# Regrouping the hidden columns of a quantized feed-forward kernel: seven waves of three pairs, the half chunk first in the last one

## The chip, the cores and the metric

The kernel runs on one core of one Trainium2 chip. The metric is the device time of one execution in microseconds (us), as the median of several runs. The core's engines appear under the profile's names: PE (matrix multiplication, with its weight loads as PEld), DVE (VectorE), ACT (ScalarE), POOL (GpSimd) and SP, whose queue issues most of the DMA transfers. PSUM, where matrix products land, has eight banks here, each of 128 partitions by 512 numbers in 32 bits.

## What is computed

The input is 2048 rows of 1024 numbers. Three layers run over it, each with a residual: a feed-forward layer, a state-space layer (a causal convolution along the 1024 numbers of each row), and the same feed-forward layer again. Each normalizes its input first.

```
x = x + 0.5 * ffn(layernorm(x))
x = x + s4(layernorm(x))             # long convolution with a computed response, plus D * u
x = x + 0.5 * ffn(layernorm(x))

ffn(x):  Wg, Wu: 1024 x 2752, Wd: 2752 x 1024, all from 4-bit words:
         W[k, n] = scale[k // 128, n] * (w4[k, n] - (zero[k // 128, n] + 1))
         h = silu(x @ Wg) * (x @ Wu);   out = h @ Wd
```

## The kernel before

**Jobs.** The rows are handled in four blocks of 512, and each block passes the feed-forward layer twice, which makes eight jobs (line 1232). A job runs an up stage, `gate_up` (line 602), then a down stage, `down` (line 678). Job 0 also turns the 4-bit words into bytes in DRAM, which all later jobs load. Job 1 also computes the tables of the convolution.

**Units and waves.** The 2752 hidden columns are 21 chunks of 128 and one half chunk of 64. A chunk has a gate column and an up column, together a pair of units; the half chunk's gate and up columns lie side by side in one unit. That is 43 units, each with a PSUM bank of its own while it is in work. A wave is a set of units that are in work together (`WAVES`, line 37): five waves of three pairs (six banks), two of two pairs (four banks), and one of two pairs and the half unit (five banks).

**Steps.** Each wave goes through the eight groups of 128 input numbers, one step for each, 64 steps in all. In a step every unit gets two products of 128x128 by 128x512 (line 628): one with the high part of the normalized input (32 bits, `xTh`) and one with the low part (16 bits, `xTl`). For the first half of the units the high product comes last, for the others the low one. After a unit's second product its bank is multiplied by the ratio of two groups' scales, in place, by ACT (line 598) for even unit numbers and by DVE (line 600) for odd ones; the half unit alternates between the two by step. The next step's product into that bank waits for this.

**End of a wave.** After a unit pair's last step `gated` (line 651) applies the sigmoid product on ACT (`g`, line 653), multiplies on DVE (`hf`, line 656) and gives both banks back. POOL then splits `hf` into a high part `hh` (line 658) and the rest `hl` (line 660). The pool of `hf` has two tiles (line 101), so a third `hf` waits for the `hl` of the first. `gated_half` (line 663) does the same for the half unit, with two more DVE operations (lines 672 and 673) in place of POOL's.

**Weights.** A step's bytes are loaded by SP (line 558) and turned into 32-bit numbers by POOL (line 576; in job 0 partly by ACT, line 574), some steps ahead: six tiles of bytes, five of weights. In job 0 `dequantize` (line 474) makes the bytes: DVE splits the words of a wave (lines 450 to 463), POOL casts eight tiles `q` from a pool of four (line 99, cast in line 478), and SP stores each of them (line 482). `dequantize_down` (line 506) does so for the down weights with the same pool.

**Down stage.** Four banks `po`, 21 chunks and the half chunk for each half of the outputs: per chunk eight products (line 689), with the banks rescaled in between as above. It takes four banks at its start.

**Hooks.** Other work is tied to step numbers (lines 1234 to 1326): moments and deviations of a normalization (lines 175 and 196, on DVE), transposes (line 219), convolutions (line 961), loads and stores of rows. For a job after a first feed-forward job the convolution of the previous block starts at step 8, in job 1 at step 38. In job 0 the words of wave w are handled from step 8w - 12 (line 520), and those of the down weights from step 52 (line 532).

**Order.** Each engine works through its own fixed order of instructions. The code sets the dependences; a scheduler puts the instructions of each engine in order when the program is built, and assigns tiles and banks. `in_order_of_writing` (line 140) fixes the order of a few pieces.

Of the kernel before, what the change touches and what calls it, by code (L numbers as in the profile page):

```python
# [12 lines left out]
I32 = mybir.dt.int32  # L13
I8 = mybir.dt.int8
U16 = mybir.dt.uint16
F32R = mybir.dt.float32r
# [7 lines left out]
P = 128  # L24
# [7 lines left out]
GK = 8  # L32
GD = 21
TW = 6
WIDE = INTER // P
HALF = INTER - WIDE * P
WAVES = [list(range(3 * w, 3 * w + 3)) for w in range(5)] + [[15, 16], [17, 18], [19, 20]]
STEPS = [(w, g) for w in range(len(WAVES)) for g in range(GK)]
NH = HID // 512
EIGHT = 8.0  # L40
LIFT = 2.0**20
# [13 lines left out]
def macaron_s4_kernel(  # L55
# [31 lines left out]
    nc = tc.nc  # L87
# [5 lines left out]
    small = ctx.enter_context(tc.tile_pool(name="small", bufs=2))  # L93
# [2 lines left out]
    hpool = ctx.enter_context(tc.tile_pool(name="h", bufs=2 * NF))  # L96
    wpool = ctx.enter_context(tc.tile_pool(name="w", bufs=5))
    bpool = ctx.enter_context(tc.tile_pool(name="bytes", bufs=6))
    qpool = ctx.enter_context(tc.tile_pool(name="q", bufs=4))
    gpool = ctx.enter_context(tc.tile_pool(name="g", bufs=3))  # L100
    hfpool = ctx.enter_context(tc.tile_pool(name="hf", bufs=2))
    ypool = ctx.enter_context(tc.tile_pool(name="y", bufs=4))
    ppool = ctx.enter_context(tc.tile_pool(name="ps", bufs=1, space=PSUM))
    dpool = ctx.enter_context(tc.tile_pool(name="dram", bufs=1, space=DRAM))
# [27 lines left out]
    def t2(name, dt=F32):  # L132
        return hpool.tile([P, 512], dt, tag="h", name=name)
# [275 lines left out]
    def units(w):  # L409
# [4 lines left out]
    width_of = lambda w: len(units(w)) * P  # L414
    w_q = [
        dpool.tile([HID, width_of(w)], I8, tag=f"wq{w}", name=f"wq{w}") for w in range(len(WAVES))
    ]
# [130 lines left out]
    loaded, made = {}, {}  # L548

    def load_bytes(i):  # L550
        j, stage, s = queue[i]
        if i == 0:
            loaded[i] = first_tile
            return
        if stage == "up":
            w, g = STEPS[s]
            loaded[i] = t = bpool.tile([P, width_of(w)], I8, tag="b", name=f"b_{j}_{s}")
            nc.sync.dma_start(t, w_q[w][bass.ts(g, P), :])
            return

        a, f = divmod(s, NF)
        loaded[i] = t = bpool.tile([P, 512], I8, tag="b", name=f"bd_{j}_{s}")
        m = width(f)
        for o in range(0, P, m):
            nc.sync.dma_start(t[o : o + m], wd_q[a][f * P : f * P + m, :])

    def make_weights(i):
        j, stage, s = queue[i]
        b = loaded.pop(i)
        made[i] = t = wpool.tile(list(b.shape), F32R, tag="w", name=f"w_{stage}_{j}_{s}")  # L570
        if i == 0:
            nc.vector.tensor_copy(t, b)  # L572
        elif j == 0 and stage == "up" and s % GK in (1, 2, 5):
            nc.scalar.copy(t, b)
        else:
            nc.gpsimd.tensor_copy(t, b)  # L576

    at_use = [0]

    def next_weights():  # L580
        i = at_use[0]
        at_use[0] += 1
        for k in range(LOAD) if i == 0 else ():
            load_bytes(k)
        for k in range(MAKE) if i == 0 else ():
            make_weights(k)
        if i + LOAD < len(queue):
            load_bytes(i + LOAD)
        if i + MAKE < len(queue):
            make_weights(i + MAKE)  # L590
        return made.pop(i)
# [10 lines left out]
    def gate_up(j, b, hooks):  # L602
        hi, lo = pieces[b]
        ps = {}
        for s, (wi, g) in enumerate(STEPS):
            w = next_weights()
            for hook in hooks.get(s, ()):
                hook()
            fs = WAVES[wi]
            n = len(fs)  # L610
            order = [(2 * f + i, i * n + u) for u, f in enumerate(fs) for i in range(2)]
            if wi == len(WAVES) - 1:
                order.append((2 * WIDE, 2 * n))


            early = len(order) // 2
            turns = [(k, pos, k == 1) for k in range(2) for pos in range(early)]
            turns += [(k, pos, k == 0) for k in (1, 0) for pos in range(early, len(order))]
            for k, pos, done in turns:
                unit, col = order[pos]  # L620
                if g == 0 and unit not in ps:
                    ps[unit] = acc(f"pg_{j}_{unit}")
                p = ps[unit]
                weights = w[:, bass.ts(col, P)]
                if k == 0:

                    weights = weights.bitcast(BF16).rearrange("p (n k) -> p k n", k=2)[:, 1, :]
                nc.tensor.matmul(  # L628
                    p,
                    weights,  # L630
                    (lo, hi)[k][:, g, :],
                    start=(g == 0 and not done),
                    stop=(g == GK - 1 and done),
                    skip_group_check=True,
                )
                if not done:
                    continue
                if g < GK - 1:
                    on_act = unit % 2 == 0 or (j == 0 and pos == 1 and g % 4 == 0)
                    if unit == 2 * WIDE:  # L640
                        on_act = g % 2 == 0
                    scaled(on_act, p, p, rat[:, unit, g : g + 1])
                elif unit == 2 * WIDE:
                    gated_half(j, ps[unit])
                    give_back(ps.pop(unit))
                elif unit % 2:
                    gated(j, unit // 2, ps[unit - 1], ps[unit])
                    give_back(ps.pop(unit - 1), ps.pop(unit))
        pieces.pop(b)
# [372 lines left out]
    def general():  # L1022
# [22 lines left out]
        def gather_table(dst, s_dram, z_dram, groups, n, name):  # L1045


            s = t4(f"s_{name}")[:, :n]
            nc.gpsimd.memset(s, 0.0)
            for k in range(3):  # L1050
                nc.sync.dma_start(s[32 * k : 32 * k + groups, :], s_dram)
            z = small.tile([P, P], I32, tag="z", name=f"z_{name}")[96:P, : n // 8]
            nc.gpsimd.memset(z, 0)
            nc.sync.dma_start(z[:groups, :], z_dram)
            zi = s[96:P, :].bitcast(I32).rearrange("p (a k) -> p k a", k=8)
            for k in range(8):
                nc.vector.tensor_scalar(
                    zi[:, k, :], z, 4 * k, 15, ALU.logical_shift_right, ALU.bitwise_and
                )
            nc.vector.tensor_scalar(dst[96:P, :], s[96:P, :].bitcast(I32), 1.0, None, ALU.add)  # L1060
            nc.vector.tensor_copy(dst[0:96, :], s[0:96, :])
            for k in range(1, 3):
                for lo in range(k, 3):
                    rows = slice(32 * lo, 32 * lo + 32)
                    nc.vector.tensor_tensor(s[rows, :], s[rows, :], dst[rows, :], ALU.subtract)
                    nc.vector.tensor_copy(dst[rows, :], s[rows, :])
# [167 lines left out]
    def fast():  # L1234
        for j, (b, k) in enumerate(JOBS):
            prev = JOBS[j - 1] if j else None
            after = JOBS[j + 1] if j + 1 < len(JOBS) else None
            up, dn = {}, {}

            def at(hooks, s, f):  # L1240
                hooks.setdefault(s, []).append(f)

            if prev:
                pb, pk = prev
                for t in range(NT):
                    at(up, t, lambda t=t: back(pb, 1, t))
                if pk == 1:
                    late = 30 if j == 1 else 0
                    at(up, 4, lambda: moments(pb, 2))
                    at(up, 5, lambda: deviations(pb, 2))  # L1250
                    s4x, s4n = {}, {}

                    def norm(t):
                        s4n[t] = normalized(pb, t)

                    def swap(t):
                        s4x[t] = turn_whole(s4n.pop(t), f"st_{pb}_{t}")

                    def conv(t):
                        convolve(pb, t, s4x.pop(t), f"{pb}_{t}")  # L1260

                    for t in range(NT):
                        at(up, late + 8 + 4 * t, lambda t=t: norm(t))
                        at(up, late + 10 + 4 * t, lambda t=t: swap(t))
                        at(up, late + 12 + 4 * t, lambda t=t: conv(t))
                    at(up, late + 27, lambda: moments(pb, 3))
                    at(up, late + 28, lambda: deviations(pb, 3, LIFT))

                    def save():
                        for t, dst in enumerate(saved(pb)):  # L1270
                            nc.sync.dma_start(dst, x[pb][t])

                    at(up, late + 28, save)
                else:

                    def store():
                        for t, dst in enumerate(rows_of(out, pb)):
                            nc.sync.dma_start(dst, x[pb][t])
                        x.pop(pb)

                    at(up, 4, store)
# [190 lines left out]
```

## Time and profile before

| what | value |
|---|---|
| median of 3 runs | 2197.08 us (2196.97 to 2197.81) |
| the profiled execution | 2195.57 us |
| its span, first to last instruction | 2193.7 us |
| mean granted PE clock | 0.993 |
| PE busy | 2119.6 us, 97% |
| DVE, ACT, POOL busy | 78%, 64%, 46% |
| DMA queue q1, share of 16 engines | 19.4% |
| one product in the up stage (line 628): 5504 of them | mean 444 and 384 ns from start to end, high and low part |
| POOL cast of a step's weights, 768 / 640 / 512 columns | 841 / 750 / 618 ns |

The profile is one execution, so its own time of 2195.57 us is what sums made from it are compared with; it lies 1.5 us under the median. A product's duration runs from its start to the end of its result and overlaps its neighbours: on a PE without waits the next product starts about 0.22 to 0.23 us later, and a PE that looks busy can still lose time. Where a stage's pace matters, starts are compared, not durations. "Idle before" in a list of groups names what ended an engine's idle time; on an engine that isn't the bottleneck such idle time costs nothing.

### The profile page before, as it was taken

Reading aid. Unit: us, or ns where it says so; the run is one execution under the profiler, and the core shown is the slowest. Engines: PE = TensorE matmul, PEld = TensorE weight load, DVE = VectorE, ACT = ScalarE, POOL = GpSimd, SP = SyncE. Lnnn points to the kernel's source line nnn. Section 1 sums busy time; section 2 is a strip of 40 time slices with the busy share of each in tenths; the row PEclk is TensorE's granted clock in tenths of the full one; section 3 lists DMA queues with packets and bytes.
Section 4 is the critical chain, followed back from the end, with each engine's and each line's share of the span. In section 5 each row is a group of like instructions: output and inputs, shape, how many; then the busy total and the mean of one; then the engine's idle time right before and its main releaser. Section 6 shows DMA issues by size and latency. Waiting matters only on the chain.

```text
span 2193.7 us, 29717 instructions
## 1 busy us (share of the span) xinstructions
PE 2119.6 (97%) x9524; PEld 1421.1 (65%) x9524; DVE 1720.4 (78%) x2826; ACT 1404.9 (64%) x2197; POOL 1015.0 (46%) x1334
## 2 busy tenths in 40 slices
PE   5999899999999999999999999999999999999998
PEld 3555665566867568655775558676686766865576
DVE  7889889778887877778777787867778677777776
ACT  5877466446754677666767667646776466767765
POOL 3868734444334453455334553435534345345642
PEclk9999999999999999999999999999999999999999
DMA  4433321112111211211321121112111121121111
GB/s 139 120 96 111 105 69 32 54 49 74 38 40 46 93 45 46 79 34 33 107 71 46 31 71 35 41 51 72 37 34 42 49 93 36 54 81 36 33 33 57
DMA packets 163681, 132.43 MB, mean 60 GB/s; under 512 B 22395, under 2 KB 151172, under 8 KB 163518
## 3 DMA queue, kind: packets, MB, share of 16 engines
q1 hardware_dynamic: 162670, 129.12, 19.4%
q8 instruction: 77, 1.26, 0.2%
q10 hardware_dynamic: 592, 1.25, 0.1%
q14 instruction: 86, 0.70, 0.1%
q0 software_dynamic: 256, 0.10, 0.0%
HBM read 104.79 MB, written 25.50 MB: 59 GB/s over the span
## 4 chain that ended last, share of the span: by engine, by line
PE 84%; DVE 7%; POOL 4%; issue 2%; DMA 1%; SPq 1%; ACT 0%; POOLq 0%; DVEq 0%; ACTq 0%
PE pg L628 50%; PE po L689 26%; PE pc L987 3%; DVE pg L600 2%; PE pc L968 1%; PE pb L711 1%; POOL hl L660 1%; PE pt L219 1%; DVE po L600 1%; DVE hf L656 1%; POOL w_up L576 1%; PE st L219 1%; POOL w_down L576 1%; POOL hh L658 1%; DVE rawd L461 0%
## 5 line engine op out<-in xcount | busy, mean ns | idle before, releaser
L598 ACT ACTIVATE pg<-pg,rat 128x512 f32<-128x512 f32 x1224 | 778.6, 660 | 472.3 <-PE pg L628 471.3
L600 DVE TENSOR_TENSOR pg<-pg,rat 128x512 f32<-128x512 f32 x1184 | 788.0, 694 | 167.5 <-PE pg L628 163.2
L628 PE MATMUL pg<-xTh,w_up 128*128 128x512 f32 x2752 | 878.5, 444 | 11.9 <-DVE pg L600 9.4
L628 PE MATMUL pg<-xTl,w_up 128*128 128x512 f16 x2752 | 731.1, 384 | 14.7 <-DVE w_up L572 6.6
L576 POOL CAST w_up<-b 128x768 fp32r<-128x768 int8 (+2 forms) x487 | 376.0, 774 | 614.0 <-PE pg L628 470.6
L628 PEld LDWEIGHTS pg<-xTh,w_up 128*128 128x128 f32 x2752 | 519.7, 190 | 203.0 <-DVE pg L600 41.7
L689 PE MATMUL po<-hl,w_down 128*128 128x512 f32 x1344 | 540.6, 405 | 15.4 <-DVE po L600 9.7
L598 ACT ACTIVATE po<-po,ratd 128x512 f32<-128x512 f32 x640 | 421.4, 662 | 175.1 <-PE po L689 175.1
L689 PE MATMUL po<-hh,w_down 128*128 128x512 f32 x1344 | 523.6, 393 | 0.0
L600 DVE TENSOR_TENSOR po<-po,ratd 128x512 f32<-128x512 f32 x640 | 441.6, 698 | 93.6 <-PE po L689 89.1
L628 PEld LDWEIGHTS <-w_up 128*128 128x128 bf16 x2752 | 228.3, 99 | 344.1 <-issue 165.2
L576 POOL CAST w_down<-bd 128x512 fp32r<-128x512 int8 x352 | 220.6, 628 | 422.3 <-PE po L689 366.2
L689 PEld LDWEIGHTS po<-hl,w_down 128*128 128x128 f32 x1344 | 252.9, 189 | 94.1 <-DVE po L600 23.9
L689 PEld LDWEIGHTS po<-hh,w_down 128*128 128x128 f32 x1344 | 254.0, 189 | 46.0
L660 POOL TENSOR_TENSOR hl<-hf,hh 128x512 fp32r<-128x512 f32 x168 | 218.0, 1297 | 7.9
L656 DVE SCALAR_TENSOR_TENSOR hf<-pg,rat,g 128x512 f32<-128x512 f32 x168 | 124.2, 749 | 86.7 <-ACT g L653 44.6
L653 ACT ACTIVATE g<-pg,rat 128x512 f32<-128x512 f32 x168 | 111.0, 687 | 45.9 <-PE pg L628 36.3
L658 POOL CAST hh<-hf 128x512 fp32r<-128x512 f32 x168 | 104.7, 623 | 61.4 <-PE pg L628 41.1
L182 DVE BATCH_NORM_STATS2 stats<-x 128x6 f32<-128x512 f32 x96 | 63.6, 677 | 1.0
L219 PE MATMUL pt<-ident,xn 128*128 128x128 f32 x256 | 44.2, 293 | 10.3 <-ACT xn L1339 7.6
L242 DVE TENSOR_TENSOR xTl<-pt,xTh 128x512 f16<-128x512 f32 x56 | 38.3, 688 | 13.7 <-ACT xTh L241 12.9
L219 PEld LDWEIGHTS pt<-ident,xn 128*128 128x128 f32 x256 | 34.8, 151 | 21.1 <-ACT xn L1339 9.2
(163 smaller groups left out, 957.2 us busy)
## 6 DMA issues: line engine op xcount, KB each, us to landing
b<-wq SPq DMA_DIRECT2D x319, 96.0 KB
bd<-wdq SPq DMA_DIRECT2D x336, 64.0 KB
x<-in_L_attn_u_dram SPq DMA_DIRECT2D x30, 512.0 KB
b<-wq SPq DMA_DIRECT2D x128, 64.0 KB
xs<-x SPq DMA_DIRECT2D x16, 512.0 KB
x<-xs SPq DMA_DIRECT2D x16, 512.0 KB
out_dram<-x SPq DMA_DIRECT2D x16, 512.0 KB
b<-wq SPq DMA_DIRECT2D x64, 80.0 KB
```

The source lines that it names most:

```text
L182: nc.vector.bn_stats(stats[:, t, i, :], x[b][t][:, bass.ts(i, 512)])
L219: nc.tensor.transpose(ps[:, bass.ts(k, P)], n[:, bass.ts(k, P)], ident)
L576: nc.gpsimd.tensor_copy(t, b)
L598: nc.scalar.activation(dst, src, AF.Copy, scale=sc)
L600: nc.vector.tensor_tensor(dst, src, sc.to_broadcast([P, TB]), ALU.mult)
L628: nc.tensor.matmul(p, weights, (lo, hi)[k][:, g, :], start=(g == 0 and not done), stop=(g == GK - 1 and done), skip_group_check=True,)
L653: nc.scalar.activation(g, pg, AF.Silu, scale=rat[:, 2 * f, GK - 1 :])
L656: nc.vector.scalar_tensor_tensor(hf, pu, last, g, ALU.mult, ALU.mult)
L658: nc.gpsimd.tensor_copy(hi, hf)
L660: nc.gpsimd.tensor_tensor(lo, hf, hi.bitcast(F32), ALU.subtract)
L689: nc.tensor.matmul(ps[c], w[:, bass.ts(c, P)], part, start=(f == 0 and k == 0), stop=(f == NF - 1), skip_group_check=True,)
L987: nc.tensor.matmul(dst, lhsT, rhs, start=start, stop=stop, skip_group_check=True)
```

## The change

The 21 pairs are taken as seven waves of three. The last wave also has the half unit, so it holds seven banks, and the half unit is the first in its order instead of the last. A step's weight tile then has at most 768 columns, also in the last wave: the half unit's weights for all eight steps come from one further load and two POOL casts into tiles of their own (`half_weights`), asked for twelve steps before the end of the up stage. There are 56 steps in place of 64.

The pool of `hf` gets a third tile. The pool of `q` loses one of four. The step numbers of the hooks follow: in job 1 the convolution starts at step 33 with a tile every three steps, in the other jobs the moments after it come at step 26 in place of 27. Job 0's words are handled from step 8w - 12 as before, now of seven waves, and those of the down weights from step 44. A small tile of the fallback path, which isn't taken here, moves to another pool.

```diff
-WAVES = [list(range(3 * w, 3 * w + 3)) for w in range(5)] + [[15, 16], [17, 18], [19, 20]]
+WAVES = [list(range(3 * w, 3 * w + 3)) for w in range(7)]
...
-    qpool = ctx.enter_context(tc.tile_pool(name="q", bufs=4))
+    qpool = ctx.enter_context(tc.tile_pool(name="q", bufs=3))
...
-    hfpool = ctx.enter_context(tc.tile_pool(name="hf", bufs=2))
+    hfpool = ctx.enter_context(tc.tile_pool(name="hf", bufs=3))
...
             w, g = STEPS[s]
-            loaded[i] = t = bpool.tile([P, width_of(w)], I8, tag="b", name=f"b_{j}_{s}")
-            nc.sync.dma_start(t, w_q[w][bass.ts(g, P), :])
+            n = 2 * P * len(WAVES[w])
+            loaded[i] = t = bpool.tile([P, n], I8, tag="b", name=f"b_{j}_{s}")
+            nc.sync.dma_start(t, w_q[w][bass.ts(g, P), :n])
...
+    def half_weights(j):
+
+        b = t2(f"b_half_{j}").bitcast(I8)[:, : GK * P].rearrange("p (g n) -> p g n", g=GK)
+        rows = w_q[-1][:, -P:].rearrange("(g k) n -> k g n", k=P)
+        nc.sync.dma_start(b, rows)
+        got = []
+        for i in range(2):
+            t = t2(f"w_half_{j}_{i}", F32R)
+            t = t.rearrange("p (g n) -> p g n", g=4)
+            nc.gpsimd.tensor_copy(t, b[:, 4 * i : 4 * i + 4])
+            got += [t[:, g] for g in range(4)]
+        return got
...
             w = next_weights()
+            if s == len(STEPS) - GK - 4:
+                half = half_weights(j)
...
             if wi == len(WAVES) - 1:
-                order.append((2 * WIDE, 2 * n))
+                order.insert(0, (2 * WIDE, None))
...
-                weights = w[:, bass.ts(col, P)]
+                weights = half[g] if col is None else w[:, bass.ts(col, P)]
...
-            z = small.tile([P, P], I32, tag="z", name=f"z_{name}")[96:P, : n // 8]
+            z = t2(f"z_{name}").bitcast(I32)[96:P, : n // 8]
...
-                    late = 30 if j == 1 else 0
+                    o, gap = (33, 3) if j == 1 else (8, 4)
...
-                        at(up, late + 8 + 4 * t, lambda t=t: norm(t))
-                        at(up, late + 10 + 4 * t, lambda t=t: swap(t))
-                        at(up, late + 12 + 4 * t, lambda t=t: conv(t))
-                    at(up, late + 27, lambda: moments(pb, 3))
-                    at(up, late + 28, lambda: deviations(pb, 3, LIFT))
+                        s = o + gap * t
+                        at(up, s, lambda t=t: norm(t))
+                        at(up, s + 2, lambda t=t: swap(t))
+                        at(up, s + 4, lambda t=t: conv(t))
+                    done = o + 3 * gap + 6
+                    at(up, done, lambda: moments(pb, 3))
+                    at(up, done + 1, lambda: deviations(pb, 3, LIFT))
...
-                    at(up, late + 28, save)
+                    at(up, done + 1, save)
```

## The prediction

> **What bounds the kernel now.** I read the page's first and fourth parts, then the stretches of some stages, then the chain of waits at two wave ends. The page says that PE carries the time:
>
> ```profile
> span 2193.7 us, 29717 instructions
> ...
> PE 2119.6 (97%) x9524; PEld 1421.1 (65%) x9524; DVE 1720.4 (78%) x2826; ACT 1404.9 (64%) x2197; POOL 1015.0 (46%) x1334
> ...
> PE 84%; DVE 7%; POOL 4%; issue 2%; DMA 1%; SPq 1%; ACT 0%; POOLq 0%; DVEq 0%; ACTq 0%
> ```
>
> The change keeps all 5504 up products and 2752 down products. So only PE's stalls can give anything: the 7% of DVE and 4% of POOL in the chain, some 240 us at the very most, much of it in the starting phase and in job 0. The stretches say where. Cut at product starts, they are: job 7's fifth wave; its last three waves; its first 32 down products; then the last three waves of job 4 and of job 0.
>
> ```profile
> core 0: us, PE busy (x) PEld busy (x) DVE busy (x) ACT busy (x) POOL busy (x), PEclk, DMA share, GB/s
> 2028.78:2050.61 21.83, 21.83 (x98) 13.02 (x96) 16.03 (x25) 15.26 (x25) 11.12 (x15) 1.00 0.09 25
> 2050.61:2098.54 47.93, 47.42 (x209) 27.80 (x208) 35.19 (x52) 33.94 (x53) 27.98 (x38) 1.00 0.13 35
> 2098.54:2108.06 9.52, 8.77 (x34) 5.78 (x33) 7.96 (x12) 6.05 (x10) 6.19 (x8) 1.00 0.09 26
> 1251.24:1302.33 51.09, 49.43 (x210) 26.69 (x208) 44.59 (x81) 33.42 (x53) 28.95 (x38) 1.00 0.24 75
> 150.24:204.90 54.66, 51.43 (x218) 27.34 (x216) 48.98 (x76) 40.10 (x66) 46.00 (x63) 1.00 0.47 140
> ```
>
> The same 208 products take 47.93 us in job 7, 51.09 in job 4 and 54.66 in job 0. The chain at job 7's change from the fifth to the sixth wave (start, us, engine, tile) shows the mechanism:
>
> ```profile
> 2050.82 0.38 POOL hh L658
> 2051.20 0.56 POOL w_up L576
> 2051.76 1.25 POOL hl L660
> ...
> 2053.03 0.75 DVE hf L656
> 2053.78 0.62 DVE pg L600
> ```
>
> The third `hf` finds both tiles taken, waits for POOL's `hl` of the first, and holds DVE's queue; the rescaling behind it comes late, and the product after it starts 0.90 us after its predecessor instead of 0.23. The list of waits on `hf` counts 37 waits for POOL's `hl`, 37.5 us. At the down start `hf_half` is caught likewise:
>
> ```profile
> 2101.46 0.76 DVE hf_half L670
> ...
> 2102.25 0.71 DVE po L600
> ...
> 2102.98 0.64 DVE hb L672
> ...
> 2103.65 0.71 DVE po L600
> ```
>
> **What the skill says.** Perfetto Trace Analysis, Optimization Strategy: the same gap repeating on the engine that should be saturated can mean that SBUF or PSUM ran out for the next tile. The trace agrees: the gap of 0.9 us recurs at the same wave change of jobs 2, 3, 4, 5, 6 and 7. TensorE: Matmul & The Clock Gate, its specification table, calls the VectorE and ScalarE queues strict FIFO; the trace agrees, a blocked `hf` delays the `pg` behind it. DMA: Bandwidth & Descriptors, Specifications, asks for 512 B or more per transfer for line rate; the new half load moves runs of 128 B, and no row of before shows such a load.
>
> **Part 1, wave shapes, quiet jobs 2, 5, 6, 7.** In the timeline a six-unit step's 12 products take 2.70 us (first low products at 2041.86, 2044.55, 2047.25), so 0.225 each. Eight steps make 21.58; the fifth wave took 21.83, so a change between three-pair waves costs 0.25. After: one such wave, 21.6, and eight steps of 14 products, 8 x 14 x 0.225 = 25.2, plus 0.25: 47.0 against 47.93. **Gain 0.9 x 4 = 3.6 us** (0 to 4.5). This needs a last wave that isn't starved of banks. Walked through with the durations above: from the start of the sixth wave's last step, `hf` 15, 16, 17 end at 2.76, 3.51, 4.26 us (with three tiles none waits for POOL), and the new wave wants their banks at 3.14 to 4.72 us. The tightest margin is 0.46 us. With two tiles the third would miss it.
>
> **Part 2, jobs 3 and 4.** Here moments and deviations at steps 44 and 45 put about 10 us on DVE (44.59 against 35.19 busy), and the stretches are 50.32 and 51.09. In jobs 5 and 6 the same work lies in a three-pair wave and costs nothing there (21.6 us for either wave): a bank has 8 product slots between its last product and its next, against 5 in a two-pair wave. After, step 44 lies in a three-pair wave, but the tail reaches the tight last wave. I take 47.0 + 1.5 = 48.5 (47.3 to 50): 1.8 + 2.6 = **4.4 us** (1.5 to 6.5).
>
> **Part 3, down starts, jobs 1 to 7.** The first 32 products take 9.52 us in job 7 and 10.13 to 10.21 in jobs 1 to 6, which also hold eight transposes; 32 x 0.228 + 0.2 for the first is 7.5, so 2.1 is stall. In the built program's order after, DVE does `hf_half`, `hf` 18, `hb`, `hf` 19, `hb`, `hf` 20, then `po`: 0.76 + 0.75 + 0.64 + 0.75 + 0.81 + 0.75 = 4.46 us ahead of the first `po`. `hf_half` can start 1.82 us into the last step (its product comes first, and the sigmoid takes 0.69), so that `po` ends at about 7.0; PE, which starts down at 3.15, wants it at 5.9. Stall 1.1 in place of 2.1, 0.7 to 1.0 where transposes fill it. **Gain 1.0 x 7 = 7 us** (2 to 9). POOL's order (three `hh`, `hl` pairs, 5.7 us, between `w_down` casts) serves each cast over 2 us early.
>
> **Part 4, job 1.** Its last three waves take 79.54 us with four convolutions. In job 5 two waves with four take 74.3, 30.7 over two plain ones, so 48.8 are left here: 0.9 over job 7, 1.8 over 47.0. The `hf` wait also sits in its chain at the fourth wave's end (`hl` 1.68 us, then no product until 425.75), some 1.5 us, and I add 1.2 for stalls around the table work, since its whole up stage takes 24.1 us more than job 5's (213.7 against 189.6) and the table products only some 12 of these. Convolutions now come at steps 37 to 46; the table they need was ready at 430.8 us, about step 35, so they don't wait. **Gain 4.5 us** (2 to 8), the down start apart.
>
> **Part 5, job 0.** DVE is 90% and POOL 84% busy in its last stretch. Three `hf` tiles, longer steps and the earlier split of the last words (DVE) help, perhaps 4 us of the 6.7 over job 7. Against it stands the smaller `q` pool: a cast of 0.84, an issue of 0.33 and a landing of 2.0 us (both from the rows of `q`) are 3.2 us; with four tiles that is 0.80 per cast, no slower than the cast, with three 1.06. Over 48 casts on POOL 0.22 x 48 = 10.6 us, which POOL's gaps in the earlier waves cover (busy 14 to 19 of 22 to 24 us per wave); uncovered it costs up to 10. **Gain 2 us** (-6 to +7).
>
> **Moved at no cost.** Half load and casts: per job one load and 2 x 0.62 on POOL; but 16 x 0.84 + 1.24 = 14.7 us replaces 16 x 0.62 + 8 x 0.75 = 15.9, and POOL idles 20 of 47.93 us. In the built order the load stands ahead of that for step 51 and the casts beside those for steps 46 and 47, so even a doubled landing of 4 us holds only casts that are more than two steps early; if not, about 3 us per job. SP issues 17 loads in place of 24. One spare bank in the last wave instead of three: no hook there takes one in the built order. Wider tiles keep each load's runs at 768 B.
>
> **Sum.** 3.6 + 4.4 + 7 + 4.5 + 2 = 21.5. From the profiled 2195.57 (span 2193.7 and 1.9 around it) that gives 2174.1; the median lies 1.5 higher, so 2175.6, and I say **2175**.
>
> **Rivals.** *Half eaten:* the last wave holds seven of eight banks, so any DVE lateness over 0.46 us goes to PE at its start, and in jobs 0, 1, 3, 4 DVE is late. Parts 2, 4, 5 give a third of 10.9, part 3 half: 3.6 + 3.6 + 3.5 = 10.7, so 2186. For it: DVE's 44.59 of 51.09; against: the built order runs ACT's units ahead there. *No change:* a product that PE starts earlier waits at the next rescaling, since DVE at 78% paces it: 2197. Against: the waves without stalls run at 0.225 with the same DVE share. *Slower:* the `q` ring of three in job 0. If every cast of `q` and of the down words (0.61 + 0.33 + 2.0 over 3 is 0.98 against 0.61, so 0.37 x 48 = 17.8) pays in full, 10.6 + 17.8 = 28.4 eats 23.5 of gains elsewhere with some left: about 2202. It decides once casts come more than three in a row with POOL as the limit, as from 225 to 270 us, where POOL is busy 37.82 of 45. *Larger:* job 0 gains 15 us and job 1 8: 21.5 + 13 + 3.5 = 38, so 2159; for it, DVE's 90% there, against, its work stays.
>
> **Chances.** Forecast 0.60, half eaten 0.20, no change 0.06, slower 0.07, larger 0.07. Range 2160 to 2192: it leaves out the slower and unchanged cases and most of the larger, 0.2. The forecast's own range is 2163 to 2184. A difference under 0.2% (4.4 us) is about what a measurement can't tell from none: faster 0.87, same 0.06, slower 0.07.
>
> **What would show it.** After: `hf` no longer waits for `hl`; the last two waves of job 7 take 47.0 us, of job 4 about 48.5; the first 32 down products 8.6 in job 7 and 9.2 in job 3; POOL's `q` waits for stores without PE waiting for `w_up`. Wrong if products at the last wave's start wait for a bank, or if job 0 grows.

## The result, and the profile after

The changed kernel takes 2183.39 us (median of 4 runs, 2179.01 to 2185.12), the kernel before on the same chip 2197.02: a ratio of 0.9939, 95% interval 0.9927 to 0.9952, 13.6 us less. In a second set, on another occasion, it was 2182.21 against 2194.26, 0.9946 (0.9932 to 0.9959). The prediction said 2175, with 2160 to 2192 as the range. So the sign and the range held, and 8 of the 22 us forecast are missing. The profiled execution took 2179.01 us, the fastest of its four and the one with the highest mean granted clock (0.993, the others 0.989 to 0.992), so its trace shows a gain of 16.6 us in span.

First the page of the changed kernel, the same three lines as before:

```profile
span 2177.1 us, 29446 instructions
...
PE 2099.9 (96%) x9524; PEld 1429.2 (66%) x9524; DVE 1718.5 (79%) x2824; ACT 1394.9 (64%) x2190; POOL 1009.5 (46%) x1281
...
PE 86%; DVE 6%; DMA 3%; POOL 2%; issue 2%; ACT 1%; SPq 0%; ACTq 0%; POOLq 0%; DVEq 0%
```

The chain has two hundredths more of PE and of DMA, two less of POOL and one less of DVE, and no engine's work has changed by much: as forecast, this is about stalls. Where they went is read from the same stretches as before, cut at product starts: job 7's sixth wave, its last two waves, its first 32 down products; the first 32 down products of job 3; the last two waves of job 4 and of job 0.

```profile
core 0: us, PE busy (x) PEld busy (x) DVE busy (x) ACT busy (x) POOL busy (x), PEclk, DMA share, GB/s
2013.42:2035.00 21.58, 21.58 (x98) 13.11 (x97) 16.11 (x25) 15.25 (x25) 11.99 (x15) 1.00 0.14 38
2035.00:2081.45 46.45, 46.45 (x209) 28.43 (x208) 34.24 (x52) 33.15 (x53) 24.12 (x30) 1.00 0.12 30
2081.45:2091.40 9.95, 8.10 (x34) 5.94 (x33) 7.89 (x12) 5.76 (x10) 8.44 (x10) 1.00 0.07 18
1046.60:1057.12 10.52, 9.12 (x42) 6.51 (x41) 8.44 (x14) 6.58 (x11) 8.64 (x11) 1.00 0.65 213
1242.92:1291.65 48.73, 47.90 (x210) 27.41 (x208) 44.34 (x81) 33.05 (x53) 24.12 (x30) 1.00 0.16 46
150.53:203.84 53.31, 49.09 (x217) 28.72 (x216) 47.07 (x73) 36.82 (x59) 42.26 (x55) 1.00 0.34 97
```

In job 7's waves PE is now busy all of the time (46.45 of 46.45 us, against 47.93 with 47.42 busy). Job 4's last waves took 48.73 where 48.5 was forecast. But the first 32 down products got slower, 9.95 us against 9.52 in job 7 and 10.52 against 10.20 in job 3, where 8.6 and 9.2 were forecast. Job 3's stretch in the kernel before was:

```profile
1054.13:1064.33 10.20, 9.12 (x43) 6.55 (x41) 8.46 (x13) 6.82 (x11) 6.18 (x8) 1.00 0.30 93
```

The timeline of job 7's down start shows it, DVE's queue first, then POOL's and the late product of PE (start, us, engine, line, operation; in brackets the idle time before it and who ended it):

```profile
2080.42 0.76 DVE L686 SCALAR_TENSOR_TENSOR hf_half<-pg,rat,g_half 64x512 f32<-64x512 f32 x1 [0.84 <-issue]
2081.21 0.75 DVE L672 SCALAR_TENSOR_TENSOR hf<-pg,rat,g 128x512 f32<-128x512 f32 x1
2081.99 0.42 DVE L688 CAST hb<-hf_half 64x512 fp32r<-64x512 f32 x1
2082.45 0.75 DVE L672 SCALAR_TENSOR_TENSOR hf<-pg,rat,g 128x512 f32<-128x512 f32 x1
2083.23 0.76 DVE L689 TENSOR_TENSOR hb<-hf_half,hb 64x512 fp32r<-64x512 f32 x1
2085.16 0.75 DVE L672 SCALAR_TENSOR_TENSOR hf<-pg,rat,g 128x512 f32<-128x512 f32 x1 [1.17 <-POOL hl L676]
2085.83 1.28 DVE L614 TENSOR_TENSOR po<-po,ratd 128x512 f32<-128x512 f32 x2
```

```profile
2082.02 0.86 POOL L674 CAST hh<-hf 128x512 fp32r<-128x512 f32 x1 [2.61 <-DVE hf L672]
2082.84 0.61 POOL L577 CAST w_down<-bd 128x512 fp32r<-128x512 int8 x1
2083.41 1.72 POOL L676 TENSOR_TENSOR hl<-hf,hh 128x512 fp32r<-128x512 f32 x1
```

```profile
2086.57 0.50 PE L705 MATMUL po<-hl,w_down 128*128 128x512 f32 x1 [1.85 <-DVE po L614]
```

The order on DVE is the one that the prediction walked through. The last `hf`, chunk 20's, could have started at 2084.0, but starts 1.17 us later, behind POOL's `hl` of chunk 18. Four products want a tile here (the half unit's, 18, 19, 20) and there are three: chunk 20's takes that of chunk 18. The first `po` rescales stand behind it in DVE's queue, and PE loses 1.85 us. The list of waits on `hf` has one such wait per job left. It gives us in total and times, here of the kernel before and of the changed one:

```profile
  POOL hl L660: 37.5, 37
...
  POOL hl L676: 9.4, 8
```

### The profile page after: what moved, and what is told of

It reads as the page before. It is cut to its first block, busy times and chain, and to the rows that moved or that the text cites. A ratio compares the mean times of both kernels' runs of the same rounds, so it can differ in the third digit from the quotient of the medians.

```text
span 2177.1 us, 29446 instructions
## 1 busy us (share of the span) xinstructions
PE 2099.9 (96%) x9524; PEld 1429.2 (66%) x9524; DVE 1718.5 (79%) x2824; ACT 1394.9 (64%) x2190; POOL 1009.5 (46%) x1281
## 4 chain that ended last, share of the span: by engine, by line
PE 86%; DVE 6%; DMA 3%; POOL 2%; issue 2%; ACT 1%; SPq 0%; ACTq 0%; POOLq 0%; DVEq 0%
PE pg L644 51%; PE po L705 27%; PE pc L1003 3%; DVE pg L614 2%; PE pc L984 1%; PE pb L727 1%; PE pt L219 1%; POOL hl L676 1%; PE st L219 1%; POOL w_down L577 1%; DVE hf L672 0%; DVE stats L182 0%; POOL hh L674 0%; DMA zd<-zd_dram 0%; DVE po L614 0%
## 5 line engine op out<-in xcount | busy, mean ns | idle before, releaser
L612 ACT ACTIVATE pg<-pg,rat 128x512 f32<-128x512 f32 x1220 | 769.6, 660 | 465.1 <-PE pg L644 464.1
L644 PE MATMUL pg<-xTh,w_up 128*128 128x512 f32 x2688 | 805.8, 430 | 9.1 <-DVE pg L614 7.8
L644 PE MATMUL pg<-xTl,w_up 128*128 128x512 f16 x2688 | 705.9, 383 | 13.5 <-DVE w_up L573 8.9
L577 POOL CAST w_up<-b 128x768 fp32r<-128x768 int8 x426 | 357.4, 842 | 564.9 <-PE pg L644 417.9
L644 PEld LDWEIGHTS pg<-xTh,w_up 128*128 128x128 f32 x2688 | 507.8, 189 | 158.2 <-DVE pg L614 18.3
L729 DVE TENSOR_TENSOR x<-x,pb 128x512 f32<-128x512 f32 x64 | 43.1, 678 | 5.6 <-PE pb L727 5.6
```

What stands on the lines that cost most here:

```text
L612: nc.scalar.activation(dst, src, AF.Copy, scale=sc)
L644: nc.tensor.matmul(p, weights, (lo, hi)[k][:, g, :], start=(g == 0 and not done), stop=(g == GK - 1 and done), skip_group_check=True,)
```

## The experiments

A pool whose tiles are taken in turn is called a ring here.

**Theory:** the gain comes from the third `hf` tile and from the waves, and the half unit's early product eats one of the three tiles at each down start, which costs about 1.1 us in each of eight jobs. **Rivals:** the down start is set by VectorE's own 4.5 us of work, or the gain has nothing to do with the tile. Job 0 and the slices `q` are a second question. Each run is compared with the kernel before on its own chip.

| run | `hf` / `q` tiles | waves | half unit | us (lowest to highest) | ratio, 95% interval |
|---|---|---|---|---|---|
| e7_q3 | 2 / 3 | before | last | 2200.72 (2199.13 to 2203.04) | 1.0027, 1.0016 to 1.0039 |
| e4_hf3q3 | 3 / 3 | before | last | 2177.34 (2176.64 to 2179.83) | 0.9919, 0.9906 to 0.9933 |
| e6_waves | 2 / 4 | after | first | 2187.52 (2185.38 to 2190.1) | 0.9966, 0.9954 to 0.9978 |
| e3_hf2 | 2 / 3 | after | first | 2193.81 (2189.71 to 2197.07) | 0.9991, 0.9984 to 0.9997 |
| changed, again (e9) | 3 / 3 | after | first | 2182.21 (2180.8 to 2182.87) | 0.9946, 0.9932 to 0.9959 |
| e2_q4 | 3 / 4 | after | first | 2178.25 (2174.06 to 2180.43) | 0.9916, 0.9902 to 0.9929 |
| e8_halflast | 3 / 3 | after | last | 2172.38 (2169.78 to 2174.55) | 0.9897, 0.9882 to 0.9912 |
| e1_halfy | 3 / 3 | after | first, other ring | 2170.37 (2169.97 to 2172.33) | 0.9884, 0.9869 to 0.9899 |
| e5_halfy_q4 | 3 / 4 | after | first, other ring | 2167.81 (2165.53 to 2168.52) | 0.9873, 0.9858 to 0.9888 |
| e11_latedve | 3 / 4 | after | as e5, split late on DVE | 2167.76 (2164.31 to 2168.7) | 0.9882, 0.9866 to 0.9897 |
| e10_latepool | 3 / 4 | after | as e5, split late on POOL | 2158.83 (2154.73 to 2161.92) | 0.9838, 0.9825 to 0.9852 |

### e1: the half unit's product in another ring

```diff
-        hf = hfpool.tile([P, TB], F32, tag="hf", name=f"hf_{j}_half")
+        hf = ypool.tile([P, TB], F32, tag="y", name=f"hf_{j}_half")
```

> The changed kernel with one edit: the half unit's product takes a tile of its own ring instead of one of the three product tiles of the pairs, so that only three products share three tiles around the start of the down products. Theory (the fourth product, chunk 20's, takes the tile of chunk 18's and waits for the low cast of chunk 18 on GpSimd): the waits for that cast fall from 8 with 9.4 us to about none, the first 32 down products go from 10.5 to about 9.4 us in jobs 1 to 6 and from 9.95 to about 8.9 in job 7, some 1.1 us per job, 8 to 9 us in all: a ratio to the kernel before of about 0.990. Rival (the start of down is set by VectorE's own queue or by the group of products that started earlier, and the wait lies beside it): first 32 down products stay at 10.5 and 9.95 us and the ratio stays at 0.994.

It took 2170.37 us. The waits for `hl` are gone from the list, and the first 32 down products of jobs 7 and 3 read:

```profile
2074.87:2083.62 8.75, 8.09 (x35) 5.93 (x33) 7.84 (x12) 5.76 (x10) 8.07 (x10) 1.00 0.06 17
1045.06:1054.39 9.33, 9.10 (x43) 6.51 (x41) 8.40 (x14) 6.59 (x11) 8.62 (x11) 1.00 0.70 231
```

That is 1.2 us less in each, and close to the forecast's 8.6 and 9.2. Jobs 2 to 7, from first to last product, go from 1553.9 to 1544.9 us, 9.0 less. Of these, 1.6 lie in job 2's fourth wave and are the granted clock's, not the tile's: that wave, in the changed kernel and then in e1, reads

```profile
707.55:733.29 25.74, 23.58 (x101) 13.75 (x98) 23.41 (x55) 14.65 (x23) 6.39 (x8) 0.93 0.24 70
708.88:733.02 24.14, 21.98 (x100) 13.10 (x98) 22.93 (x55) 14.58 (x23) 6.41 (x8) 1.00 0.26 74
```

e3 and e7, which don't have e1's edit, show 24.1 us there too. The rival falls as an account of the 1.2 us; what VectorE's own queue adds comes with e10. The eight down starts together got 9.5 us shorter, about three quarters of what the medians moved (12 to 13 us). The rest isn't placed: job 0 took 2 us more in this trace, at a lower granted clock (0.94 against 1.00 in its last wave but one).

### e8: the half unit last

```diff
-                order.insert(0, (2 * WIDE, None))
+                order.append((2 * WIDE, None))
```

> The changed kernel with one line: the half unit is last in the last wave, not first. Waves, rings and the half unit's own weight tiles stay. Theory (four products share three tiles whatever their order; now the half unit's product takes the tile of chunk 18's and waits for the same low cast): the wait goes over to the half unit's product, first 32 down products of jobs 1 to 6 at 10.2 to 10.8 us, ratio 0.993 to 0.996. Rival (the half unit first is what costs, by putting its bf16 pieces ahead of the other products on VectorE): first 32 down products at 9.4, ratio 0.989 to 0.990, as with another ring.

2172.38 us, a ratio of 0.9897, and the first 32 down products at 9.47 to 9.51 us in jobs 1 to 6: these are close to the rival's numbers, and the theory was wrong in size. The wait does go over to the half unit's product, but it is short:

```profile
L686 DVE SCALAR_TENSOR_TENSOR hf_half<-pg,rat,g_half x8: 756/757/757, 207.4 to 2077.3; 64x512 f32<-64x512 f32 x8
...
  POOL hl L676: 2.1, 8
```

2.1 us over eight jobs instead of 9.4. The fourth product comes later in this order, when `hl` of chunk 18 is nearly done, and the two splitting steps fall behind the first `po`. Job 7's first 32 down products take 8.80. Not four products on three tiles alone, but four with the half unit's one early is what costs. This run moves the wait and the two splitting steps at once; e1 removes the wait alone, and e10 below the steps.

### e3, e4 and e6: the tile without the waves, the waves without the tile

```diff
# e3, on the changed kernel; e6 has this and q back at 4
-    hfpool = ctx.enter_context(tc.tile_pool(name="hf", bufs=3))
+    hfpool = ctx.enter_context(tc.tile_pool(name="hf", bufs=2))
# e4, on the kernel before
-    qpool = ctx.enter_context(tc.tile_pool(name="q", bufs=4))
+    qpool = ctx.enter_context(tc.tile_pool(name="q", bufs=3))
-    hfpool = ctx.enter_context(tc.tile_pool(name="hf", bufs=2))
+    hfpool = ctx.enter_context(tc.tile_pool(name="hf", bufs=3))
```

> The changed kernel with two product tiles instead of three, nothing else. Theory (the third tile gives each of the early three-pair waves 0.2 us, and at the start of down it is used up by the half unit's product): each early wave goes from 21.6 back to 21.8 us, 43 such waves cost 8 to 9 us, the start of down gets 0 to 1 us per job slower: 8 to 17 us more than the changed kernel, ratio 0.998 to 1.002. Rival (the gain is all from the order of the waves, the third tile is worth nothing): ratio 0.994, early waves stay at 21.6.

> The kernel before with the two ring sizes of the changed kernel alone (three product tiles, three slices), its waves and its half unit left where they were. Theory: early waves get 0.2 us shorter each as in the changed kernel, 8 to 9 us in all, and the start of down, which has three products on three tiles here, up to 1 us per job; job 0 loses 2 to 4 us to the slices: ratio 0.992 to 0.997. Rival (the wave order is the gain): ratio 1.000 or more.

> The changed kernel with both rings at the sizes of before (two product tiles, four slices): the waves and the place of the half unit alone. Theory (the waves are worth about 11 us in jobs 1 to 7, as in the trace with two product tiles, and job 0's loss of 6 us there comes from the ring of three slices): 2184 to 2188 us, ratio 0.995 to 0.9965, job 0 at 284 us. Rival (job 0's loss comes from the waves themselves, whose last but one wave has 31.3 us there): 2192 to 2195 us, ratio 0.998 to 1.000, job 0 at 289 us or more.

The two ring sizes alone, with the waves left where they were, give 0.9919, 5 to 6 us under the changed kernel's medians, though the intervals still touch. That is just under the 0.992 to 0.997 expected: job 0 was to lose 2 to 4 us and took 281.0 against 284.2 in its trace. The third tile without the smaller `q` ring was not run on the old waves. The waves alone give 0.9966, and with `q` at three next to nothing (0.9991). In e6 the forecast of 2184 to 2188 held, and job 0 came to 284.6 us: its loss in e3 (290.4) belongs to the `q` ring, the one difference of the two kernels. In e3 the down start was expected to get 0 to 1 us slower per job and got 0.9 us faster. What the new waves are worth with three tiles can be read from e8 against e4: 5 us, with intervals that just touch. The kernel with both ring sizes and the old waves (e4), then that with two `hf` tiles and the new waves (e3), in job 7: an early wave, the last waves, the first 32 down products:

```profile
2011.60:2033.18 21.58, 21.58 (x98) 13.11 (x97) 16.11 (x25) 15.25 (x25) 11.12 (x15) 1.00 0.09 25
2033.18:2080.55 47.37, 47.37 (x209) 27.79 (x208) 35.13 (x52) 33.93 (x53) 27.84 (x38) 1.00 0.13 36
2080.55:2089.29 8.74, 8.49 (x35) 5.54 (x33) 7.84 (x12) 6.24 (x10) 6.52 (x8) 1.00 0.10 28
```

```profile
2026.82:2048.70 21.88, 21.88 (x98) 13.02 (x97) 16.11 (x25) 15.27 (x25) 11.96 (x15) 1.00 0.13 37
2048.70:2095.94 47.24, 46.91 (x209) 28.33 (x208) 33.95 (x52) 33.18 (x53) 24.14 (x30) 1.00 0.12 30
2095.94:2105.01 9.07, 8.21 (x35) 5.94 (x34) 8.02 (x12) 5.71 (x10) 8.33 (x10) 1.00 0.05 14
```

The early wave goes to 21.58 with the tile and stays at 21.88 without it. The last waves get 0.6 us from the tile, 0.7 from the waves, 1.5 from both. The down start is the point where the changed kernel loses: 8.74 with the tile and the old order, 9.07 with the new order and two tiles, 9.95 with both. With two tiles the scheduler puts the first `po` rescale ahead of the last two `hf`, as DVE's queue in e3 shows; with three it puts it behind them.

```profile
2097.96 0.70 DVE L614 TENSOR_TENSOR po<-po,ratd 128x512 f32<-128x512 f32 x1
2098.56 0.74 DVE L672 SCALAR_TENSOR_TENSOR hf<-pg,rat,g 128x512 f32<-128x512 f32 x1
2099.69 0.75 DVE L672 SCALAR_TENSOR_TENSOR hf<-pg,rat,g 128x512 f32<-128x512 f32 x1 [0.38 <-POOL hl L676]
```

So at the down start the third tile and the new order, with the half unit early in it, each gain and together lose. The half unit's early place was not run apart from the new waves with two tiles.

### e2 and e7: the slices of the weights

```diff
# e2, on the changed kernel
-    qpool = ctx.enter_context(tc.tile_pool(name="q", bufs=3))
+    qpool = ctx.enter_context(tc.tile_pool(name="q", bufs=4))
# e7, on the kernel before
-    qpool = ctx.enter_context(tc.tile_pool(name="q", bufs=4))
+    qpool = ctx.enter_context(tc.tile_pool(name="q", bufs=3))
```

> The changed kernel with the ring of weight slices q back at four tiles. Theory (a ring of three costs job 0 a few us, where the slices are loaded as they are needed): the waits of the slice loads for a tile fall from 10 with 11.4 us to about 2 with 3 us, job 0 gets 2 to 5 us shorter, the other jobs stay within 0.5 us, and the runs spread less than the 6 us of the changed kernel: ratio 0.991 to 0.993. Rival (job 0 is bound by VectorE's casts and the loads of the intermediate, the slices' waits lie beside that): job 0 within 1 us, ratio 0.994.

> The kernel before with three weight slices instead of four, nothing else. Theory (the slices' waits for a tile go from 2 with 2.8 us to about 10 with 12 us and some of it reaches TensorE in job 0): 2 to 4 us slower, ratio 1.001 to 1.002, job 0 at 286 to 289 us. Rival (the waits lie beside other work): ratio 1.000, job 0 within 1 us of 284.2.

The kernel before gets 5 us slower with three slices (1.0027, interval off 1), more than the 2 to 4 us expected. Job 0 took 288.8 us against 284.2 in its trace, and casts wait for a stored tile (the store's landing, us in total, times; the kernel before, then e7):

```profile
  DMA wq<-q: 2.8, 2
...
  DMA wq<-q: 13.2, 12
```

In that trace job 0's loss lies in its first 32 down products, 14.7 us against 9.8. In the chain there an `hh` stands behind casts of the down words on POOL, and the granted clock is 0.77, so part of it is the clock's.

The changed kernel gets 4 to 5 us back by the medians with four slices (0.9916 against 0.9939 and 0.9946, the first interval just touching, the second apart), job 0 3.4 us in its trace, where 3 waits with 2.7 us are left. The spread of 6 us did not get smaller (2174.06 to 2180.43); that part of the expectation was wrong. So was that the other jobs would stay within 0.5 us: job 7 took 2.4 us more, though its instructions stand in the same order as in the changed kernel. Of these, 1.6 lie in its first 32 down products, at a granted clock of 0.85 where the changed kernel's trace had 1.00:

```profile
2079.19:2090.73 11.54, 9.71 (x34) 7.13 (x33) 7.90 (x12) 5.77 (x10) 8.49 (x10) 0.85 0.09 22
```

### e9: the changed kernel once more

> The changed kernel itself, beside the others on one chip, for a time and a second trace to set them against. Theory (its runs vary by what the weight slices wait for in job 0): 2180 to 2185 us, the first 32 down products of jobs 1 to 6 again at 10.5 us, each within 0.1, while job 0 differs by over 1 us from the first trace's 281.7. Rival (the runs vary everywhere): jobs 2 to 7 differ by more than 0.3 us each.

Jobs 2 to 7 took 1553.9 us in both traces. Job 0 took 281.7 in one and 284.5 in the other, 2.3 of the difference in its up stage. So these two runs differ in job 0. Its last wave but one took 28.29 us at a granted clock of 0.94, against 27.57 at 1.00; its second wave took 23.80 against 22.59 at 1.00 in both. The clock is part of the variation, then, and what else varies stays open: the chain there has stores of `q`, loads of zero words and VectorE in turn, and no run separates them.

### e5, e10 and e11: what is left of the stall

With e1's edit PE still loses time at the down start:

```profile
2078.80 0.50 PE L705 MATMUL po<-hl,w_down 128*128 128x512 f32 x1 [0.66 <-DVE po L614]
```

It starts 1.06 us after its predecessor (2077.74) instead of about 0.23. That stall of 0.83 us is most of the 1.1 us of the prediction's walk, so its claim that 4.46 us of DVE's queue set the start can now be tried: take the two splitting steps of the half unit's product, first used at down step 21, out of that queue. e5 joins e1 and four slices; e10 and e11 start from e5.

```diff
-        nc.vector.tensor_copy(both[high], hf[high])
-        nc.vector.tensor_tensor(both[low], hf[high], both[high].bitcast(F32), ALU.subtract)
...
# in down, e10
+            if d == 3:
+                half_pieces(nc.gpsimd, j, 0)
+            if d == 3:
+                half_pieces(nc.gpsimd, j, 1)
# in down, e11
+            if d == 4:
+                half_pieces(nc.vector, j, 0)
+            if d == 8:
+                half_pieces(nc.vector, j, 1)
```

`half_pieces` holds the two removed lines, one for each part, for the engine given.

> Both edits together: the half unit's product in another ring (2170.4 us alone) and four tiles for the weight slices (2178.3 alone, job 0 3.4 us shorter in its trace). Theory (the two lie in different places, job 0 and the starts of down, so they add): 2166 to 2168 us, ratio 0.986 to 0.9875, job 0 at about 280 us between its first products and job 1's. Rival (job 0 is bound by the loads of the intermediate and by VectorE, and the 3.4 us were a difference between runs): 2170 us, ratio 0.988.

> The half unit's product in another ring and four slices, as in the kernel of 2167.8 us, and the two steps that split that product into its halves go from VectorE, ahead of the last two products, to GpSimd at down step 3; they are first used at down step 21. Theory (VectorE's queue sets the start of down: 4.46 us of work from the half unit's product to the second product of the last pair's rescale; 1.2 us less there): the 1.1 us for which TensorE waits for the second po rescale goes, first 32 down products of jobs 1 to 6 at 8.0 to 8.5 us instead of 9.3, 8 us in all: 2159 to 2161 us, ratio 0.9835 to 0.9845. Rival (GpSimd's casts for the last pair are late next, or the two steps hold up the down weights on GpSimd): 2165 us or more, ratio 0.986 or more.

> The same, but the two splitting steps stay on VectorE and move to down steps 4 and 8, one each. Theory: the start of down gets 1.1 us shorter as with GpSimd, and VectorE, which has some 0.3 us left in a down step of 1.8, gives back 0.3 to 0.8 us per job at steps 4 and 8: 2161 to 2166 us, ratio 0.984 to 0.9865. Rival (a down stage has no room on VectorE, all 1.2 us come back): 2168 us, ratio 0.987.

e5: 2167.81 us, as the theory had it, but its interval overlaps e1's and job 0 took 281.9 us in its trace where 280 was expected, so that the two edits add is likely and not shown. e10: 2158.83 us, a ratio of 0.9838 within the forecast's 0.9835 to 0.9845; the fastest kernel here, 35 us under the kernel before. Its queue on DVE at job 7's down start, and the first 32 down products of jobs 7 and 3:

```profile
2062.69 0.76 DVE L687 SCALAR_TENSOR_TENSOR hf_half<-pg,rat,g_half 64x512 f32<-64x512 f32 x1 [0.79 <-ACT g_half L685]
2063.48 2.22 DVE L673 SCALAR_TENSOR_TENSOR hf<-pg,rat,g 128x512 f32<-128x512 f32 x3
2065.62 1.28 DVE L615 TENSOR_TENSOR po<-po,ratd 128x512 f32<-128x512 f32 x2
```

```profile
2063.77:2071.44 7.67, 7.67 (x35) 6.10 (x34) 6.57 (x10) 5.79 (x10) 7.00 (x9) 1.00 0.06 17
1036.71:1045.23 8.52, 8.52 (x43) 6.75 (x41) 7.25 (x12) 6.64 (x11) 7.79 (x10) 1.00 0.69 232
```

PE is busy all of both stretches: with the two steps gone from DVE's queue the stall is gone, and nothing else is late next there. e11, the same steps late but on VectorE, gains nothing over e5. The first `po` rescale starts as early as in e10 (2.94 us after the half unit's product starts), but the stall comes back as soon as the steps run, which is 4.3 and 6.5 us into job 7's down stage, and there the cast takes twice as long in jobs 1 to 7, the subtraction in job 7 alone (ns, lowest, median, highest; in the changed kernel they had medians of 424 and 760):

```profile
L696 DVE CAST hb<-hf_half x8: 425/858/884, 215.0 to 2070.7; 64x512 fp32r<-64x512 f32 x8
L698 DVE TENSOR_TENSOR hb<-hf_half,hb x8: 686/808/1465, 220.7 to 2073.0; 64x512 fp32r<-64x512 f32 x8
```

The product of PE behind the cast starts 0.74 us after its predecessor in job 7, and the first 32 take 9.33 us there. The theory was wrong for e11, and the rival's 2168 us came: VectorE has no room for the two steps in the first down steps.

## Why the prediction was right, and where it was wrong

The parts of the sum against the two profiled executions, in us gained:

| part of the sum | forecast | traces |
|---|---|---|
| 1: last waves of jobs 2, 5, 6, 7 | 3.6 | 5.8 |
| 2: last waves of jobs 3, 4 | 4.4 | 3.8 |
| 3: down starts, jobs 1 to 7 | 7.0 | -2.4 |
| 4: up stage of job 1 | 4.5 | 3.0 |
| 5: job 0 | 2 | 2.5 |
| first five waves of jobs 2 to 7 | none | 6.3 |
| first product of job 0 | none | -2.3 |
| sum, before rounding | 21.5 | 16.6 |

That so much of the forecast gain came is in part luck: 6.3 us that the sum doesn't have made up for two thirds of the 9.4 us by which Part 3 missed. Without them some 7 us of gain would be left, still inside the range.

**The step that failed is Part 3.** It put "`hf` 20" straight behind the second `hb` and let PE stall 1.1 us in place of 2.1. The order was right, and DVE's work ahead of `po` was even shorter than reckoned (`hb` 0.42 and 0.76 us for 0.64 and 0.81). What was left out is that the half unit's product draws from the same three tiles, so that chunk 20's waits for `hl` of chunk 18; the sentence that POOL's order "serves each cast over 2 us early" looked at PE as the reader of that cast and not at DVE waiting for its tile. Part 1 had checked the tiles for three `hf`; here there are four. Sign and size are shown by e1: with one tile more, 9.33 and 8.75 us are measured where the forecast had 9.2 and 8.6. Its own sign, "`hf` no longer waits for `hl`", named the view that shows it.

**Part 1** had the mechanism and too small a size. "Plus 0.25" for a wave change was taken over from the kernel before; it was the same wait for `hl`, and is gone (46.45 us, not 47.0). For that reason the five early waves got faster too, 6.3 us that the sum doesn't have, though the 37 waits in the list were more than one per job. **Part 2** held to 0.6 us. **Part 4** came out inside its range, but not for its reasons: only 1.5 of its 4.5 us stood for the `hf` wait. Job 1's up stage took 213.8 us before, 214.6 with the waves alone (e6), 213.7 with the smaller `q` ring as well (e3), and 210.8 once the third tile was there too. Regrouping the convolutions gave nothing that these traces show; the tile gave the 3 us. **Part 5**: the net of 2 came out as 2.5 from first product to first product, and as 0.2 with the later first product counted in; in e9's trace job 0 took 284.5 us against 284.2 before, which the prediction had named as a sign of being wrong. It is a gain less some 5 us for the ring of three (e7), well inside the bound of 10.6 that it named; "which POOL's gaps cover" was too hopeful. The half unit's load and casts cost next to nothing: of eight loads one was waited for, 1.0 us.

**The rivals.** "Half eaten" at 2186 lies nearer to the median than 2175, but its cause isn't what happened: the last waves gave 9.6 us where 8.0 were forecast, and the loss was at the down start, through a tile. "Slower" through `q` had the right place and a fifth of its price of 28.4 us. The remaining 3 us between the traces' 16.6 and the medians' 13.6 belong to runs that have no trace; e9's trace puts as much into job 0, and in part to the clock. The later first product stays open too: in e7, with the smaller `q` ring alone, it came at 31.3 us against 28.8, but in e2, with four slices and the new waves, at 31.1.

## What to carry to other kernels

When a ring gets a tile more, count all of its users in the window where it is meant to help, and for the one that goes round the ring ask which engine reads last what it overwrites: here a fourth user one engine away took back what the third tile gave. A fixed-looking cost at each stage change may be the same wait that is about to be removed; it then pays everywhere, not only where it was seen to hurt. What isn't needed for a long time, as the half unit's two splitting steps, belongs neither ahead of the critical first rescale nor late on the same full engine, but on one with idle time, as e10 against e5 and e11 shows for this kernel. And before a difference of one or two us between two traces is put down to an edit, the granted clock of the stretch belongs beside it.

## What the runs showed of the hardware

VectorE and GpSimd delayed each other. In the changed kernel's job 7 VectorE's cast (2081.99, 0.42 us) went undisturbed and POOL's `hh`, started 0.03 us later, took 0.86 instead of 0.61; POOL's `hl`, started 0.18 us after VectorE's subtraction (2083.23, 0.76 us), took 1.72 instead of 1.28. In e11's job 7 POOL's `hl` had started first both times:

```profile
2070.02 1.29 POOL L677 TENSOR_TENSOR hl<-hf,hh 128x512 fp32r<-128x512 f32 x1
2070.73 0.86 DVE L696 CAST hb<-hf_half 64x512 fp32r<-64x512 f32 x1
2072.59 1.28 POOL L677 TENSOR_TENSOR hl<-hf,hh 128x512 fp32r<-128x512 f32 x1
2072.96 1.47 DVE L698 TENSOR_TENSOR hb<-hf_half,hb 64x512 fp32r<-64x512 f32 x1
```

In e11's job 0, with no work of POOL beside them, the cast and the subtraction took 0.42 and 0.69. In each of these pairs the one that started later lost time, and the earlier one lost none to it; the changed kernel's subtraction had itself lost 0.07 to a weight cast of POOL that ran for 0.22 us more. The Trainium skill, SBUF — State Buffer, section "Who interferes with whom", says that VectorE and GpSimd share a pair of ports as an exclusive lock and that the order of issue decides who waits. These traces agree in kind; the later one lost 0.07 to 0.78 us, in each case some 0.14 less than the rest of the earlier one's time. The prediction's walk had no room for this: it took `hl` at its usual 1.28 us. In the changed kernel's job 7 `hh` and `hl` of chunk 18 lost 0.69 us together, and POOL's queue had no gap between them, so by this sum, an estimate that no run tests alone, more than half of the 1.17 us for which chunk 20's `hf` waited comes from this delay.

The granted clock wasn't even within a run. In the changed kernel's trace the stretch from 713.6 to 717.0 us, in job 2's fourth wave, had half of it:

```profile
713.60:717.00 3.40, 3.40 (x10) 1.67 (x9) 2.37 (x10) 1.77 (x3) 0.00 (x0) 0.50 0.09 29
```

The wave took 25.74 us in it and 24.14 us in e1's trace, which had the whole clock there. What sets such a stretch off isn't shown here.
